# Value products placed between the matmuls of the Fourier transforms, two width groups in later rows, and value fetches on ScalarE in five rows of eight

## The chip, the cores and the metric

The kernel runs on one core of a Trainium2 chip. The metric is the device time of one execution in microseconds; the median of several runs is given. Before the change it is 3284.2 us (three runs, 3283.5 to 3284.87 us).

The core has five engines with queues of their own: TensorE (PE in the profile; PEld are its weight loads), VectorE (DVE), ScalarE (ACT), GpSimd (POOL) and SyncE (SP), which here only issues DMAs.[...]

## The reference, cut to what matters

The input x has the shape (32, 56, 56, 128): 32 images, 56 by 56 tokens, 128 channels, all in fp32. Two layers follow, each added to its input after a group norm:

```python
x = x + window_attention(group_norm(x))     # layer 0
x = x + fourier_ff(group_norm(x))           # layer 1

# window_attention: 7x7 windows, shifted by 3, 4 heads of 32 channels
qkv  = win @ w_qkv.T
attn = softmax(q @ k.T * scale + bias + mask)
out  = (attn @ v) @ w_proj.T + b_proj

# fourier_ff
out_y = einsum(dct(x along W)[:32 modes], w0)
out_x = einsum(dct(x along H)[:32 modes], w1)
h     = idct(out_x along H) + idct(out_y along W)
out   = relu(h @ W1 + b1) @ W2 + b2
```

The product attn @ v is what this document calls the values. dct(..) with 32 modes is the forward transform, idct the back transform; both are matmuls with constant matrices.

## The kernel before, in words

**Rows and cycles.** The kernel goes through the images in rows of windows: NWR = 8 rows an image, 256 rows in all. One turn of the outer loop (line 1219) is a cycle. In cycle r, attention's scores are made for row r, and values and projection for row r - 3; the softmax of the rows between runs on VectorE, GpSimd and ScalarE meanwhile. Eleven cycles after an image's first row (CONV_BEGIN = 11), its second layer begins. It is spread over 16 cycles, counted by c, which the text calls steps: in every cycle one image is at a step c from 0 to 7 and, where there is an earlier one, this is at step c + 8 (`fourier`, line 905). Cycles before 11 (`first_rows`) fill this pipeline.

**What each step of the second layer does.** Step 0: forward transform over the width, two halves h of the tokens (`transform`, lines 688 to 710). Steps 1 and 2: forward transform over the height, one half each, in two pieces. Steps 3 to 5: mixing of the modes by w1 and w0 (`mix`). Then the back transform in groups of 16 lines (`modes_back`, line 777), the last group with 8: `back_groups` (line 910) gives height groups 0 and 1 to step 5, 2 and 3 to step 6, width groups 0 and 1 to step 7, 2 and 3 to step 8. Each group is fetched from PSUM by `fetch_back`: height groups by ScalarE copies into xf, width groups by VectorE additions onto xf. Steps 8, 9, 10 and 12 to 15 are the feed-forward layer, in seven groups of up to 512 tokens (FF_AT, `ff_in`, `ff_out`).

**Order inside a cycle.** The order on PE, ScalarE, VectorE and GpSimd is written by hand (line 1201): the instructions stand on each engine as the Python code calls them. A steady cycle calls `halves_first` (qk products, first feed-forward matmuls), `half_columns` (mixing), `eighths` (values, then the forward transform), `quarters` (scores; the back transform after them where a feed-forward group runs in the same cycle, else before), `attn_max`, `last_fetch`, and `halves_last` (the v product of this row, rest of the mixing, exp, `ff_out`, projection). So on PE a steady cycle reads: qk, feed-forward in, values, forward transform, scores, back transform, v, mixing, feed-forward out, projection.

**How the matmuls sit in the array.** Tokens lie in two halves of the 128 partitions. A value product (line 546) has 49 rows, in the upper or lower row half u, and 32 columns for its head h: eight places. It is made for four pairs of windows pr, so a row has 32 value products. They run with pr outside, then h, then u, so that the halves alternate. A transform product (line 702) has 56 rows in row half r and 32 columns for its block g of channels, again eight places, r innermost. A product of the back transform (line 789) has 64 rows (li) and 64 columns (hs): four places; a group has four chunks c (the last group two), each with four products. Scores (line 477) have 64 by 64 too. All other matmuls use 128 rows and 64 columns. In the profile each fp32 product counts as two matmuls.

**Banks.** PSUM has four banks named pa for attention and four named pc for the second layer, each taken in turn. The values take two banks (po), one for each u; two banks later in turn v and the projection come to them again. ScalarE fetches u = 0 (one instruction), VectorE u = 1 (three, because of the shifted window), in lines 560 to 578. Each transform and each group of the back transform takes two pc banks.

**Loads.** `load_back` (line 915) issues on SP the loads of zT for the back groups of the next cycle; `load_columns` (line 732) those of the token columns for the height transform.

Of the kernel before, what the change touches and what calls it, by code (L numbers as in the profile page):

```python
# [1 line left out]

# [1 line left out]

# [11 lines left out]
S = 56  # L16
C = 128
WS = 7
SS = 3
NH = 4  # L20
HD = C // NH
WT = WS * WS
NWR = S // WS
# [10 lines left out]
JP = 64  # L34
# [13 lines left out]
def swin_fourier_kernel(  # L48
# [33 lines left out]
    def attn_bank():  # L82
        return bank("pa", 4)
# [447 lines left out]
        nc.vector.transpose(eT.rearrange("p t (k j) -> p k t j", k=2), blocks[r % 2])  # L531
        im.eT[i] = eT

    def attn_values(im, i, r):


        v = v_sb[r % 3]
        po = [attn_bank(), attn_bank()][::-1]
        HALF = RT // 2
        po4 = [p[:, :HALF].rearrange("p (r n s) -> p n r s", r=WS, s=WS) for p in po]  # L540
        eT = im.eT.pop(i)
        for pr in range(NP):
            for h in range(NH):
                for u in range(2):
                    ks = slice(u * JP, u * JP + WT)
                    nc.tensor.matmul(  # L546
                        po4[u][h * HD : (h + 1) * HD, pr],
                        lhsT=v[ks, pr, h * HD : (h + 1) * HD],
                        rhs=eT[ks, h * NP + pr, :WT],
                        start=True,  # L550
                        stop=True,
                    )

        if i % 2 == 0:
            im.oT = oT_sb[i // 2 % 2]
        oT = im.oT


        oTr = oT[:, i % 2 * RT : (i % 2 + 1) * RT].rearrange("p (r x) -> p r x", x=S)
        for u in range(2):  # L560
            src = po[u][:, :HALF].rearrange("p (r f x) -> p r f x", r=WS, f=NP)
            n = NP - u
            dst = bass.AP(
                oTr.tensor,
                oTr[:, :, SS + u * WS :].offset,
                [oTr.ap[0], [S, WS], [2 * WS, n], [1, WS]],
            )
            parts = [(dst, src[:, :, :n])]
            if u:
                parts += [  # L570
                    (oTr[:, :, S - WS + SS :], src[:, :, n, : WS - SS]),
                    (oTr[:, :, 0:SS], src[:, :, n, WS - SS :]),
                ]
            for d, f in parts:
                if u:
                    nc.vector.tensor_scalar(d, f, im.bias[:, 2:3], None, ALU.add)  # L576
                else:
                    nc.scalar.activation(d, f, AF.Identity, bias=im.bias[:, 2:3])  # L578
# [109 lines left out]
    def transform(im, width, h):  # L688

        if width:  # L690
            toks = [x1[:, 2 * CH * h : 2 * CH * (h + 1)]]
        else:
            toks = [im.cols.pop(2 * h + j) for j in range(2)]
        dct_sb = (dct_w if width else dct_h)[:, :, 0]
        py = [conv_bank(), conv_bank()]
        at = 0
        for tok in toks:
            n = tok.shape[1] * KB
            for g in range(C // KB):
                cs = slice(g * KB, (g + 1) * KB)  # L700
                for r, ps in enumerate(LINE):
                    nc.tensor.matmul(  # L702
                        py[r][cs, at : at + n],
                        lhsT=dct_sb[ps],
                        rhs=tok[ps, :, cs],
                        start=True,
                        stop=True,
                    )
            at += n
        im.py[width, h] = py  # L710

    def turn_modes(im, width, h):

# [63 lines left out]
    def modes_back(im, width, g):  # L777

        if not width and g == 0:
            im.xf = big.tile([P, S, S], F32, tag="xf", name="xf", bufs=2)  # L780
        zT = im.zT.pop((width, g))
        idct = idctw if width else idcth.rearrange("p h r -> p (h r)")
        l0, n = LINES[g]
        nch = n // 4
        px = [conv_bank(), conv_bank()]
        for c in range(nch):
            for li, ls in enumerate(HALVES):
                for hs in HALVES:
                    nc.tensor.matmul(  # L789
                        px[li][hs, c * 2 * S : (c + 1) * 2 * S],  # L790
                        lhsT=zT[ls, c, hs],
                        rhs=idct[ls, :],
                        start=True,
                        stop=True,
                    )
        im.px[width, g] = px

    def fetch_back(im, width, g):

# [109 lines left out]

    def back_groups(c):  # L910

        if c in (5, 6, 7, 8):
            return [(c >= 7, (c + 1) % 2 * 2 + j) for j in range(2)]
        return []

    def load_back(cycle):
        for im, c in fourier(cycle):
# [75 lines left out]
    def has_ff(cycle):  # L993
        return any(c in FF_AT for _, c in fourier(cycle))
# [9 lines left out]
                for g in (2 * c - 8, 2 * c - 7):  # L1004
                    mix(im, True, g)

    def quarters(cycle):
        def back():
            for im, c in fourier(cycle):
                for j, (width, g) in enumerate(back_groups(c)):  # L1010
                    modes_back(im, width, g)
                    if not (c == 8 and j):
                        fetch_back(im, width, g)

        if not has_ff(cycle):
            back()
        im, i = row(cycle)
        if im:
            attn_scores(im, i, cycle)
        if has_ff(cycle):  # L1020
            back()

    def eighths(cycle):
        im, i = row(cycle - 3)
        if im:
            attn_values(im, i, cycle - 3)
        for im, c in fourier(cycle):
            if c == 0:
                for h in range(2):
                    transform(im, True, h)  # L1030
                    turn_modes(im, True, h)
                next(im.stats)
            if c == 1:
                for r in range(2):
                    scale_modes(im, True, 1, r)
                shift_modes(im, True)
            if c in (1, 2):
                transform(im, False, c - 1)
                if c == 1:
                    for g in range(2):  # L1040
                        load_columns(im, g + 2)

    def last_fetch(cycle):
        for im, c in fourier(cycle):
            if c == 8:
                fetch_back(im, *back_groups(c)[1])

    def columns_turn(cycle):
        for im, c in fourier(cycle):
# [60 lines left out]
                ff_out(im, FF_AT.index(c))  # L1110

    EARLY = (0, 3, 4, 5, 7)

    def halves_last(cycle):
        im, i = row(cycle)
# [29 lines left out]
    def first_rows(cycle):  # L1145
        im, i = row(cycle)
        im3, i3 = row(cycle - 3)
        if im:
            attn_qk(im, i)
        if cycle == NWR:  # L1150
            norm_step(cycle)
        last, j = row(cycle - 4)
        if last:
            attn_sums(last, j)
        if cycle >= NWR:
            next_quarter(cycle)
        if cycle:
            attn_exp(cycle - 1)
        if im3:
            attn_values(im3, i3, cycle - 3)  # L1160
        tokens_bias(cycle)
        if im:
            attn_scores(im, i, cycle)
            attn_max(cycle)
        if last:
            attn_squares(last, j)
            add_sums(last, j)
        divide(cycle)
        turn(cycle)
        if im3:  # L1170
            attn_project(im3, i3)
        if cycle in (0, NWR - 1):
# [12 lines left out]
        next_groups(cycle)  # L1185
        if cycle == NWR - 2:
            for _ in range(2):
                norm_step(NWR - 1)
        if 1 < cycle < 10:
            mix_weights(cycle - 2)  # L1190
        if cycle in (6, 7):
            back_weights(cycle - 6)
        if cycle == 8:
            ff_weights()
        if cycle == CONV_BEGIN - 1:
            attn_sums(im3, i3)
            attn_squares(im3, i3)
            attn_exp(cycle)

    ET = mybir.EngineType  # L1200
    with tc.manual_schedule(engines={ET.PE, ET.Activation, ET.DVE, ET.Pool}):
# [17 lines left out]
        for cycle in range(NB * NWR + CONV_BEGIN + FF_AT[-1] - NWR + 1):  # L1219
# [4 lines left out]
            if not row(cycle - 3)[0]:  # L1224
                eighths(cycle)
                columns_turn(cycle)
                behind_max(cycle)
                half_columns(cycle)
                half_columns(cycle, True)
                scale_first(cycle, 0)  # L1230
                scale_first(cycle, 1)
                load_first(cycle)
                last_out(cycle)
                quarters(cycle)
# [6 lines left out]
            quarters(cycle)  # L1241
            if row(cycle)[0]:
                attn_max(cycle)
            last_fetch(cycle)
# [66 lines left out]
```

## Time and profile before

| what | value |
|---|---|
| median of three runs | 3284.2 us (3283.5 to 3284.87) |
| the profiled execution | 3282.72 us, its span 3280.9 us |
| mean granted TensorE clock | 0.991 |
| value products, L546 | 16384 matmuls, busy 209.3 us |
| forward transform, L702 | 3072 matmuls, busy 59.3 us (width) and 72.9 us (height) |
| back transform, L789 | 7168 matmuls, busy 107.1 us (width) and 99.6 us (height) |
| scores, L477 | 8192 matmuls, busy 234.5 us |
| VectorE fetch of values, L576 | 768 instructions, 171.5 us |
| ScalarE fetch of values, L578 | 256 instructions, 117.2 us |

The busy time of a group of matmuls is that of the union of its instructions, whose ends are modelled, so it is no measure of how well the array is filled. A row of a steady cycle takes about 3280.9 us over 256 rows, some 12.8 us, the fill and the end of the pipeline included. A line of the timeline gives the start, the time from the first start to the last end, engine, line, operation and tiles, and the number of instructions.

### The profile page before, as it was taken

What the parts mean: (1) busy time and instruction counts of PE and PEld (TensorE: products, weight loads), DVE (VectorE), ACT (ScalarE), POOL (GpSimd) and SP (SyncE); (2) the same over time, 40 slices, a digit from 0 to 9 for tenths busy, and PEclk for the clock granted to TensorE, in tenths of its full rate; (3) what the DMA queues carried; (4) which work ended last, traced back from release to release, by engine and by line L of the source; (5) the groups of instructions that cost most, each with busy time, mean ns of one, the idle gap of its engine ahead of it and who ended that gap; (6) DMA issues with size and microseconds to landing.
All of it is one profiled execution on the core that took longest, in us unless ns stands there. A gap on an engine that the chain in (4) does not pass through costs nothing.

```text
span 3280.9 us, 151050 instructions
## 1 busy us (share of the span) xinstructions
PE 3154.8 (96%) x65408; PEld 2394.1 (73%) x65408; DVE 2637.5 (80%) x5066; ACT 2100.4 (64%) x3680; POOL 2346.8 (72%) x2634
## 2 busy tenths in 40 slices
PE   4689999999999999999999999999999999999999
PEld 3467777777777777777777777777777777777776
DVE  8788888888888888888888888888888888888751
ACT  3456766666766666666666766666666666666663
POOL 7777777777777677777777777777777777777741
PEclk9799999999999999999999999999999999999999
DMA  6546556565556555656556656656565656565453
GB/s 115 106 119 147 137 138 144 136 143 146 137 134 142 137 142 143 142 135 146 137 144 145 141 134 143 137 141 144 136 140 136 146 131 146 140 143 136 121 140 96
DMA packets 1168157, 448.39 MB, mean 137 GB/s; under 512 B 520106, under 2 KB 1137628, under 8 KB 1167492
## 3 DMA queue, kind: packets, MB, share of 16 engines
q1 hardware_dynamic: 1158148, 433.18, 55.7%
q8 instruction: 514, 8.42, 1.1%
q10 hardware_dynamic: 8736, 5.38, 0.7%
q14 instruction: 151, 1.24, 0.1%
q0 software_dynamic: 608, 0.17, 0.0%
HBM read 276.97 MB, written 161.48 MB: 134 GB/s over the span
## 4 chain that ended last, share of the span: by engine, by line
PE 83%; ACT 7%; DVE 3%; DMA 2%; issue 2%; SPq 2%; POOL 0%; ACTq 0%; DVEq 0%; POOLq 0%
PE pc L113 38%; PE pa L113 10%; PE pa L455 7%; PE pc L789 5%; PE pa L591 5%; PE pc L750 5%; PE pa L477 5%; PE pa L546 4%; PE pc L702 3%; ACT hid L833 2%; ACT k L442 2%; SPq L760 1%; ACT xr L628 1%; ACT z L758 1%; DMA zscr<-z 1%
## 5 line engine op out<-in xcount | busy, mean ns | idle before, releaser
L521 POOL TENSOR_TENSOR blocks<-a,rs 128x512 f32<-128x512 f32 x1506 | 1280.5, 857 | 399.2 <-DVE rs L509 251.2
L113 PE MATMUL pc<-wff,hid 128*64 128x128 f32 x12544 | 742.0, 273 | 2.6 <-ACT hid L833 1.0
L113 PE MATMUL pc<-xf,wff 128*64 128x512 f32 (+2 forms) x3584 | 718.5, 539 | 1.0 <-DVE xf L807 0.9
L113 PEld LDWEIGHTS pc<-wff,hid 128*64 128x64 f32 x12544 | 706.5, 137 | 15.7 <-ACT hid L833 5.3
L496 POOL TENSOR_TENSOR a<-a,mx 128x784 f32<-128x784 f32 x251 | 377.7, 1505 | 358.6 <-DVE mx L495 341.6
L113 PEld LDWEIGHTS pc<-xf,wff 128*64 128x64 f32 x3584 | 278.6, 136 | 356.8 <-issue 249.6
L833 ACT ACTIVATE hid<-pc,b1sb 128x512 f32<-128x512 f32 (+2 forms) x896 | 500.5, 643 | 41.1 <-PE pc L113 41.1
L113 PE MATMUL pa<-xw,wn 128*64 128x392 f32 x2048 | 399.9, 501 | 29.6 <-ACT wn L411 29.6
L462 ACT COPY v<-pa 128x512 f32<-128x512 f32 x256 | 151.9, 593 | 414.7 <-PE pa L455 411.7
L485 DVE TENSOR_TENSOR a<-pa,bm 128x392 f32<-128x392 f32 x502 | 260.0, 559 | 90.2 <-PE pa L477 70.8
L442 ACT ACTIVATE k<-pa,bqkv,heads 128x392 f32<-128x392 f32 x512 | 319.0, 674 | 14.9 <-PE pa L113 1.1
L840 POOL TENSOR_TENSOR res<-res,b2sb 128x512 f32<-128x512 f32 (+2 forms) x256 | 265.7, 1044 | 85.0 <-DMA res<-scr 85.0
L725 ACT ACTIVATE y<-modes,rstd 128x448 f32<-128x448 f32 x256 | 276.3, 1137 | 71.5 <-DVE modes L718 64.0
L531 DVE STREAM_TRANSPOSE eT<-blocks 128x1024 f32<-128x1024 f32 x256 | 313.4, 1224 | 0.9 <-POOL blocks L521 0.9
L502 ACT ACTIVATE a<-a 128x784 f32<-128x784 f32 x251 | 214.9, 856 | 151.1 <-POOL a L496 150.9
L455 PE MATMUL pa<-wn,xw 128*64 128x128 f32 x4096 | 289.1, 283 | 22.0 <-ACT oT L578 16.4
L127 POOL TENSOR_TENSOR xr<-xr,bproj 128x384 f32<-128x384 f32 (+1 forms) x256 | 292.6, 1143 | 20.6 <-DMA xr<-in_x_dram 7.9
L546 PEld LDWEIGHTS pa<-eT,v 49*32 49x32 f32 x16384 | 173.6, 106 | 161.1 <-ACT hid L833 48.7
L432 ACT ACTIVATE q<-pa,bqkv 128x392 f32<-128x392 f32 x256 | 149.3, 583 | 220.7 <-PE pa L113 219.0
L576 DVE TENSOR_SCALAR oT<-pa,bqkv 128x147 f32<-128x147 f32 (+2 forms) x768 | 171.5, 279 | 140.5 <-PE pa L546 138.3
L507 DVE TENSOR_REDUCE sm<-a 128x16 f32<-128x784 f32 x251 | 240.9, 960 | 40.2 <-ACT a L502 40.1
L591 PE MATMUL pa<-wproj,oT 128*64 128x128 f32 x3584 | 249.9, 275 | 23.3 <-DVE oT L576 21.1
(108 smaller groups left out, 4975.3 us busy)
## 6 DMA issues: line engine op xcount, KB each, us to landing
zscr<-z SPq DMA_DIRECT2D x512, 112.0 KB
xin<-in_x_dram SPq DMA_DIRECT2D x496, 112.0 KB
htok<-scr SPq DMA_DIRECT2D x256, 196.0 KB
zT<-zscr SPq DMA_DIRECT2D x192, 256.0 KB
res<-scr SPq DMA_DIRECT2D x160, 256.0 KB
out_dram<-res SPq DMA_DIRECT2D x160, 256.0 KB
scr<-x SPq DMA_DIRECT2D x256, 112.0 KB
xr<-in_x_dram SPq DMA_DIRECT2D x256, 84.0 KB
```

Source lines behind the costliest of these rows:

```text
L113: nc.tensor.matmul(dst[ps], lhsT=lhsT[:, ps], rhs=rhs, start=start, stop=stop)
L127: nc.gpsimd.tensor_tensor(piece, piece, bproj.unsqueeze(1).to_broadcast([P, n, C]), ALU.add)
L442: nc.scalar.activation(k_sb[:, u], pk[:, :RT].rearrange("p (w j) -> p w j", j=WT), AF.Identity, bias=im.bias[:, 3 + u : 4 + u], scale=head ...
L455: nc.tensor.matmul(pv[HALVES[w % 2], w // 2 * C : (w // 2 + 1) * C], lhsT=im.half[i // NP][:, t0 : t0 + JP], rhs=im.w[:, 2 * C : 3 * C], s ...
L496: nc.gpsimd.tensor_tensor(a3, a3, mx.unsqueeze(2).to_broadcast([P, 2 * NWR, WT]), ALU.subtract)
L521: nc.gpsimd.tensor_tensor(dst[to, k, :, :n], a3[src, :, kb * KB : kb * KB + n], rs[src].unsqueeze(2).to_broadcast([src.stop - src.start, 2 ...
L531: nc.vector.transpose(eT.rearrange("p t (k j) -> p k t j", k=2), blocks[r % 2])
L546: nc.tensor.matmul(po4[u][h * HD : (h + 1) * HD, pr], lhsT=v[ks, pr, h * HD : (h + 1) * HD], rhs=eT[ks, h * NP + pr, :WT], start=True, sto ...
L591: nc.tensor.matmul(pp[hs, (n - n0) * C : (n - n0 + 1) * C], lhsT=oT[:, t0 : t0 + JP], rhs=wproj, start=True, stop=True,)
L725: nc.scalar.mul(y[:, r], t.rearrange("p (n k) -> p n k", k=NM), im.rstd)
L833: nc.scalar.activation(hf[:, :n], ph[:, :n], AF.Relu, bias=b1sb[:, f : f + 1])
L840: nc.gpsimd.tensor_tensor(im.res[:m, c0:c1], im.res[:m, c0:c1], b2sb[:m].unsqueeze(1).to_broadcast([m, c1 - c0, C]), ALU.add,)
```

## The change

Four things are changed.

1. Values, forward transforms and back transforms no longer run their own loops: each returns its products as two lists, one for each row half, of parts. A new function `beside` emits them: a part of the other work on row half 0, then value products on row half 1, then the other work on row half 1, then value products on row half 0, until the first piece of the other work is through. What remains follows in the old manner, one part at a time and both halves of it. Where there is no other work, all values are emitted with u = 1 ahead of u = 0. How many pairs of windows go into one place depends on the parts of the first piece: four (all) beside the width transform, two beside a half of the height transform and beside the short last back group, one beside a full back group.
2. The back transform is therefore called ahead of the scores in all rows. Width groups 2 and 3 leave step 8 and go one each to steps 11 and 12, where they are fetched in `last_fetch`; the second group of step 7 is fetched there too.
3. The value fetches are emitted after all of these products. In rows with cycle % 8 of 2, 3, 5, 6 or 7, which are steps 7, 0, 2, 3 and 4, ScalarE fetches both halves (four instructions), in the order 0, 1; in the others VectorE's three for u = 1 come first. The half u = 0 now has the first of the two banks.
4. Turning and scaling of modes, and the loads of the columns of step 1, follow both pieces instead of standing between them.

```diff
-    def attn_values(im, i, r):
+    def values(im, i, r):
         v = v_sb[r % 3]
-        po = [attn_bank(), attn_bank()][::-1]
+        po = [attn_bank(), attn_bank()]
...
-        for pr in range(NP):
-            for h in range(NH):
-                for u in range(2):
-                    ks = slice(u * JP, u * JP + WT)
-                    nc.tensor.matmul(
...
+        def product(u, pr, h):
+            ks = slice(u * JP, u * JP + WT)
+            nc.tensor.matmul(
...
+        return [
+            [[partial(product, u, pr, h) for h in range(NH)] for pr in range(NP)]
+            for u in range(2)
+        ]
+
+    def fetch_values(im, i, both=False):
...
-        for u in range(2):
+        for u in (0, 1) if both else (1, 0):
...
-                if u:
+                if u and not both:
                     nc.vector.tensor_scalar(d, f, im.bias[:, 2:3], None, ALU.add)
                 else:
                     nc.scalar.activation(d, f, AF.Identity, bias=im.bias[:, 2:3])
...
+        return [
+            [[partial(product, j, r, g) for g in range(C // KB)] for j in range(len(toks))]
+            for r in range(2)
+        ]
...
+        return [
+            [[partial(product, c, li, hs) for hs in HALVES] for c in range(nch)]
+            for li in range(2)
+        ]
...
     def back_groups(c):
 
-        if c in (5, 6, 7, 8):
-            return [(c >= 7, (c + 1) % 2 * 2 + j) for j in range(2)]
-        return []
+        if c in (5, 6, 7):
+            return [(c == 7, (c + 1) % 2 * 2 + j) for j in range(2)]
+        return [(True, c - 9)] if c in (11, 12) else []
...
+    def beside(mine, others):
+
+        def emit(parts):
+            for part in parts:
+                for product in part:
+                    product()
+
+        n = max(len(other[0]) for other in others) if others else 0
+        steps = [(other, k) for other in others for k in range(len(other[0]))]
+        if not mine:
+            for other, k in steps:
+                for r in range(2):
+                    emit(other[r][k : k + 1])
+            return
+        first = len(others[0][0]) if others else 0
+        if n == 1:
+            steps, first = steps, 1
+        share = NP // first if first else NP
+        for k in range(first):
+            other, at = steps[k]
+            emit(other[0][at : at + 1])
+            emit(mine[1][k * share : (k + 1) * share])
+            emit(other[1][at : at + 1])
+            emit(mine[0][k * share : (k + 1) * share])
+        if not first:
+            for pr in range(NP):
+                for u in (1, 0):
+                    emit(mine[u][pr : pr + 1])
+        for other, k in steps[first:]:
+            for r in range(2):
+                emit(other[r][k : k + 1])
 
     def eighths(cycle):
-        im, i = row(cycle - 3)
-        if im:
-            attn_values(im, i, cycle - 3)
+        last, i = row(cycle - 3)
+        mine = values(last, i, cycle - 3) if last else []
+        others = []
+        for im, c in fourier(cycle):
+            if c == 0:
+                others += [transform(im, True, h) for h in range(2)]
+            if c in (1, 2):
+                others.append(transform(im, False, c - 1))
+            for width, g in back_groups(c):
+                others.append(modes_back(im, width, g))
+        beside(mine, others)
+        if last:
+            fetch_values(last, i, cycle % NWR in VALUES_BY_ACT)
...
+            if c in (5, 6, 7):
+                for width, g in back_groups(c)[: 1 if c == 7 else 2]:
+                    fetch_back(im, width, g)
 
     def last_fetch(cycle):
         for im, c in fourier(cycle):
-            if c == 8:
-                fetch_back(im, *back_groups(c)[1])
+            if c in (7, 11, 12):
+                fetch_back(im, *back_groups(c)[-1])
...
+    VALUES_BY_ACT = (2, 3, 5, 6, 7)
```

More of the change, by code (lines that the diff above doesn't have):

```diff
@@ L1 @@
 from contextlib import ExitStack
+from functools import partial
 import numpy as np
@@ L541, in attn_values @@
         eT = im.eT.pop(i)
-        for pr in range(NP):
-            for h in range(NH):
-                for u in range(2):
-                    ks = slice(u * JP, u * JP + WT)
[L546 to L552, printed above, removed]
+        im.po = po
+        def product(u, pr, h):
+            ks = slice(u * JP, u * JP + WT)
+            nc.tensor.matmul(
+                po4[u][h * HD : (h + 1) * HD, pr],
+                lhsT=v[ks, pr, h * HD : (h + 1) * HD],
+                rhs=eT[ks, h * NP + pr, :WT],
+                start=True,
+                stop=True,
+            )
+        return [
[3 more added lines that the diff above has]
+    def fetch_values(im, i, both=False):
+        po = im.po
+        HALF = RT // 2
         if i % 2 == 0:
@@ L695, in transform, with product @@
         py = [conv_bank(), conv_bank()]
-        at = 0
-        for tok in toks:
+        im.py[width, h] = py
+        def product(j, r, g):
+            tok, ps, cs = toks[j], LINE[r], slice(g * KB, (g + 1) * KB)
             n = tok.shape[1] * KB
[L699 to L710, printed above, removed]
+            nc.tensor.matmul(
+                py[r][cs, j * n : (j + 1) * n],
+                lhsT=dct_sb[ps],
+                rhs=tok[ps, :, cs],
+                start=True,
+                stop=True,
+            )
+        return [
+            [[partial(product, j, r, g) for g in range(C // KB)] for j in range(len(toks))]
+            for r in range(2)
+        ]
     def turn_modes(im, width, h):
@@ L785, in modes_back, with product @@
         px = [conv_bank(), conv_bank()]
[L786 to L795, printed above, removed]
-        im.px[width, g] = px
+        im.px[width, g] = px
+        def product(c, li, hs):
+            nc.tensor.matmul(
+                px[li][hs, c * 2 * S : (c + 1) * 2 * S],
+                lhsT=zT[HALVES[li], c, hs],
+                rhs=idct[HALVES[li], :],
+                start=True,
+                stop=True,
+            )
+        return [
+            [[partial(product, c, li, hs) for hs in HALVES] for c in range(nch)]
+            for li in range(2)
+        ]
     def fetch_back(im, width, g):
@@ L1005, in half_columns, with scores @@
                     mix(im, True, g)
[L1007 to L1016, printed above, removed]
+    def scores(cycle):
         im, i = row(cycle)
@@ L1019, in quarters @@
             attn_scores(im, i, cycle)
-        if has_ff(cycle):
-            back()
-    def eighths(cycle):
-        im, i = row(cycle - 3)
-        if im:
-            attn_values(im, i, cycle - 3)
+    def beside(mine, others):
[27 more added lines that the diff above has]
+                emit(other[r][k : k + 1])
+    def eighths(cycle):
+        last, i = row(cycle - 3)
[11 more added lines that the diff above has]
+            fetch_values(last, i, cycle % NWR in VALUES_BY_ACT)
         for im, c in fourier(cycle):
@@ L1029, in eighths @@
                 for h in range(2):
-                    transform(im, True, h)
                     turn_modes(im, True, h)
@@ L1036, in eighths @@
                 shift_modes(im, True)
[L1037 to L1041, printed above, removed]
+                for g in range(2):
+                    load_columns(im, g + 2)
+            if c in (5, 6, 7):
+                for width, g in back_groups(c)[: 1 if c == 7 else 2]:
+                    fetch_back(im, width, g)
     def last_fetch(cycle):
         for im, c in fourier(cycle):
-            if c == 8:
-                fetch_back(im, *back_groups(c)[1])
+            if c in (7, 11, 12):
+                fetch_back(im, *back_groups(c)[-1])
     def columns_turn(cycle):
@@ L1159, in first_rows @@
         if im3:
-            attn_values(im3, i3, cycle - 3)
+            beside(values(im3, i3, cycle - 3), [])
+            fetch_values(im3, i3)
         tokens_bias(cycle)
@@ L1233, in swin_fourier_kernel @@
                 last_out(cycle)
-                quarters(cycle)
                 last_fetch(cycle)
@@ L1240, in swin_fourier_kernel @@
             eighths(cycle)
-            quarters(cycle)
+            scores(cycle)
             if row(cycle)[0]:
```

## The prediction, made before the changed kernel was run

> **What bounds the kernel now.** I read the page first, then the list of waits on PE, then the timeline of PE inside single rows, because the page says that PE decides and only the timeline shows how its stages follow each other. From the page:
>
> ```profile
> PE 3154.8 (96%) x65408; PEld 2394.1 (73%) x65408; DVE 2637.5 (80%) x5066; ACT 2100.4 (64%) x3680; POOL 2346.8 (72%) x2634
> PE   4689999999999999999999999999999999999999
> ...
> PEclk9799999999999999999999999999999999999999
> ...
> PE 83%; ACT 7%; DVE 3%; DMA 2%; issue 2%; SPq 2%; POOL 0%; ACTq 0%; DVEq 0%; POOLq 0%
> ```
>
> PE is busy in nine tenths or more of every slice after the third, at full granted clock, and carries 83% of the chain of waits. PE is idle 126 us in all (3280.9 - 3154.8), most of it in the first three slices. What is left in the steady part is small; the list of waits names it:
>
> ```profile
> PE pa L113 <- ACT wn L411: 29.6, 2, 24.4
> ...
> PE pa L455 <- ACT oT L578: 16.4, 30, 1.0
> ```
>
> The first line is the start. The second comes once an image (30 times, 0.55 us each), in the row of Fourier step 4, where the v product waits until ScalarE has fetched the values out of its bank. So a microsecond more or less of PE work in a row is nearly a microsecond of the span, and the question is what the new order of matmuls costs on PE. The timeline of PE in one row of step 7 (values L546, scores L477, back transform L789, v L455):
>
> ```profile
> 1591.82 0.81 PE L546 MATMUL pa<-eT,v 49*32 49x49 f32 x64
> 1592.56 0.91 PE L477 MATMUL pa<-k,q 64*64 64x98 f32 x32
> 1593.28 1.71 PE L789 MATMUL pc<-idctw,zT 64*64 64x112 f32 x64
> 1594.92 1.09 PE L455 MATMUL pa<-wn,xw 128*64 128x128 f32 x16
> ```
>
> "49*32" is rows times columns of the array that a matmul holds. Compare each start with the modelled end (start plus length) of the line above. Scores and back transform are both 64*64: the second starts 0.19 us before the first ends. Values to scores is 64x32 to 64x64 (49 rows lie in a half of 64), back to v is 64x64 to 128x64: there the next starts only 0.07 us before the end. The values and the forward transform (L702) have one size, and run into each other; the transform and the scores do not:
>
> ```profile
> 1603.55 0.76 PE L546 MATMUL pa<-eT,v 49*32 49x49 f32 x61
> 1604.11 0.56 PE L702 MATMUL pc<-x,dct_w 56*32 56x448 f32 x1
> 1604.12 0.20 PE L546 MATMUL pa<-eT,v 49*32 49x49 f32 x1
> 1604.12 0.56 PE L702 MATMUL pc<-x,dct_w 56*32 56x448 f32 x1
> 1604.14 0.22 PE L546 MATMUL pa<-eT,v 49*32 49x49 f32 x2
> 1604.16 1.77 PE L702 MATMUL pc<-x,dct_w 56*32 56x448 f32 x30
> 1605.86 0.91 PE L477 MATMUL pa<-k,q 64*64 64x98 f32 x32
> ```
>
> Transform matmuls start in rounds of eight, 376 ns apart, for 448 columns: 0.84 ns a column. With that rate I took, over the whole trace, the time from the end of the last matmul's streaming to the start of the next stage. Where the size stays it is zero or below (-36 ns from values to transform). Where it changes it is 92 to 96 ns at the median, every time: 157 changes from values to scores 92 ns, 93 from transform to scores 92 ns, 192 from 128x64 to values 96 ns. And it is the whole array that waits: the first scores matmul sits on the upper left quarter, the last transform matmul on the last columns of the lower half, and the scores still wait for that one.
>
> [...]the first scores matmul after a change is 295 ns long and later ones 243 (52 ns exposed for 64 columns), the first value matmul 228 against 203 (25 ns for 32). [...]above, transform matmuls start before the last value matmuls, so something here passes others on other tiles.[...]
>
> **The change, part by part.**
>
> *Back transform and values, interleaved.* In rows of step 5, 6, 7, 3 and 4 the new order is: two back products on row half 0 (64x64), values on row half 1 (64x32), two back products on half 1, values on half 0, and again. Every hand-over changes the size, so nothing lies beside anything. The length of such a piece:
> - Two back products are four matmuls (each fp32 product is two[...]). Exposed load 53 ns, two rounds of 94 ns (112 columns at 0.84), 7 ns for the second product's later start (starts in a round are 6.7 ns apart), 92 ns change: 340 ns with rounding.
> - Four value products: 25 ns load, two rounds of 41 ns, 20 ns for four starts, 92 ns: 220 ns (222 taken).
> - One step is two of each: 1.124 us; four steps are 4.50 us.
>
> Before, the same work took 0.735 us (values with the change after it, 1591.82 to 1592.56) and eight rounds of 95 ns, 0.76 us (one group of the back transform). So such a row grows by 4.50 - 0.735 - 0.76 = 3.00 us. The second group of steps 5 to 7 follows in one piece, as before. Step 4 has the short group (two chunks): two steps, with eight value products a piece (some 313 ns: four value rounds), 2 x 2 x (0.340 + 0.313) = 2.61 us, before 0.735 + 0.38; it grows by 1.50 us. Values of another image run beside steps 5 to 7 of 31 images and beside steps 3 and 4 (reached a whole image later) of 30: 31 x 3 x 3.00 + 30 x (3.00 + 1.50) = 279 + 135 = +414 us.
>
> *Transform and values, interleaved.* One size, so the two halves can work at once. Step 0: before, 2.22 us (1603.55 to 1605.86 less the change). After, each half has two transforms of 2 x 0.376 and its values, 4 x 0.082, in a row, some 1.9 to 2.0 us with the starts: -0.25 us. Steps 1 and 2: before, 1.65 us (1618.20 to 1619.94 less 0.09); after, 4 x 0.188 + 0.33 = 1.08 a half, 1.35 with starts and instruction supply: -0.3 us each. 31 x 0.85 = -26 us. From both sides: nothing excludes that the values wait behind the transform's second pass; then the pieces lie one after another (rival 3).
>
> *Two width groups moved from step 8 to steps 11 and 12.* The same matmuls, and two fetches by VectorE (612 ns each, 375 for the short one), in rows where PE decides as well: nothing by itself. Their users come later: tokens 1536 to 2047 are used in step 12, and tokens from 2560 in step 14. The loads of zT, two a group on SP, go one group a row; in steps 5 to 7 the first group is wanted some 1.5 us sooner after its issue (5.3 us instead of 6.8 in the row above). The back transform waited for such a load 0.5 us in the whole run; I take nothing, up to 20 us. The loads of htok for step 1 are issued behind both pieces of values; SP has no wait before PE's list.
>
> *Values fetched by ScalarE in five rows of eight.* VectorE loses three instructions, 371 + 237 + 230 = 0.84 us; ScalarE gains three, at 458 ns for 196 elements and 342 ns for 56 (L578, L730) some 1.1 us, about 170 us in all. What stands behind them on ScalarE is v's copy (L462), which waited 414.7 us for PE: they are covered. The v product now waits for the first fetch alone (0.46 us), under the scores' 0.73 us. Cost nothing; without the cover up to 0.6 us in 160 rows.
>
> *A wait that goes.* In step 4's row ScalarE gets 1.5 us more before v is due: the 16.4 us go, and nothing is late next, PE being the later one.
>
> Sum: 414 - 26 - 16 = +372 us on 3282.7 us (the profiled execution; its span is 3280.9), 3654; the median of the runs is 1.5 us above, so **3655 us**.
>
> **The rivals.**
> 1. *Clock falls.* An interleaved stretch is 4.5 us long and PE streams in half of it, on half the array. The clock record moves in steps of 3.41 us; reckoned as streaming time, steps with 0.39 or less were followed by half clock, steps with 0.42 or more were not. Half of the time is above; counted by array area it would be a quarter, below. Then some 0.72 of 123 rows would lose 1.7 to 3.4 us: 3805 to 3955, middle 3880 us.
> 2. *The other side: no drain between different halves.* If the change of size costs only where tiles overlap, values and back run beside each other: 1.09 + 0.09 us a row instead of 1.495, -0.31 us. 31 x 3 x 0.31 + 30 x 0.62 = 47, with 26 of the transforms: 3284 - 73 = 3211 us. It decides where a step of two back and two value pieces takes under 0.374 us (1.495 over 4), against 1.124. For it: no hand-over of before is between disjoint tiles alone. Against: the scores' start above waits for a disjoint tile.
> 3. *Transform and values don't overlap.* Step 0 gains 0.7 us instead of losing, steps 1 and 2 0.77 each: 31 x (2.24 + 0.85) = +96 us, 3750 us.
>
> **How the numbers follow.** Chances: the forecast 0.68, clock 0.16, no overlap 0.08, no drain 0.07, no measurable change 0.01. The forecast's own range is 3600 to 3710 (10 ns on each of 123 x 16 changes are 20 us; the transforms' gain may be 0 to 1.5 us an image; ScalarE's waits may stay). The range to 3840 takes in rival 3 and the low end of rival 1. A difference of 0.2%, 6.6 us, is what can be told from none: faster 0.07, within 0.01, slower 0.92.
>
> **What would show it.** Right: in the timeline of a step 5 row, sixteen alternating groups of L789's and L546's successors of about 0.34 and 0.22 us, 4.5 us together, rows of steps 0 to 2 slightly shorter, granted clock still 0.99, and more VectorE and ScalarE idle time in rows of steps 3 to 7 that ends with PE. Wrong: back and value matmuls that start within each other's groups (rival 2); PEclk under 9 in all slices (rival 1); transform groups that start only after the value group ended (rival 3).

## The result, and the profile after

The changed kernel takes 3924.5 us (median of four runs, 3921.5 to 3929.4); the kernel before, run beside it, 3284.5 us. The ratio is 1.195, with a 95% interval of 1.193 to 1.196. The direction was forecast and the size was not: 3655 us, with a range up to 3840, were predicted. The profiled execution has a span of 3922.8 us against 3280.9, and a mean granted clock of 0.925 against 0.991.

The page of the kernel after, the lines that answer to those shown of before (line numbers have moved: values L545, back transform L799, scores L478, v L456, forward transform L709):

```profile
PE 3805.6 (97%) x65408; PEld 2767.9 (71%) x65408; DVE 2503.6 (64%) x4601; ACT 2217.7 (57%) x4145; POOL 2341.7 (60%) x2634
...
PE   4699999999999999999999999999999999999999
...
PEclk9899999999899989899999999998998998989989
```

PE has as many instructions as before and is as full, over a span that is 642 us longer. VectorE lost 134 us of work and ScalarE gained 117; with PE as the bound neither shows in the time. What is new is the third line: the granted clock dips again and again, where before it stood at 9 from the third slice on. The trace's clock record, which lists the stretches at full and at half clock, has 592 us at half clock, before 64 us.

The timeline of PE in a row of step 5 that fell wholly into full clock:

```profile
1494.67 0.41 PE L799 MATMUL pc<-idcth,zT 64*64 64x112 f32 x4
1495.01 0.29 PE L545 MATMUL pa<-eT,v 49*32 49x49 f32 x8
1495.23 0.41 PE L799 MATMUL pc<-idcth,zT 64*64 64x112 f32 x4
1495.57 0.29 PE L545 MATMUL pa<-eT,v 49*32 49x49 f32 x8
1495.79 0.41 PE L799 MATMUL pc<-idcth,zT 64*64 64x112 f32 x4
...
1499.15 1.00 PE L799 MATMUL pc<-idcth,zT 64*64 64x112 f32 x32
1499.97 0.85 PE L478 MATMUL pa<-k,q 64*64 64x98 f32 x32
```

These are single instructions merged into groups: first the back transform's piece on one row half, then the values on the other, and so on. Read the starts: 0.34 us from a back piece to a value piece, 0.22 us to the next back piece, 1.12 us for a step of two and two (1494.67 to 1495.79). No interleaved group starts inside another by more than the 0.07 us that stands for a full stop. Over the whole trace the median pause, from the end of the last matmul's streaming to the next start, reckoned as in the prediction, is 93 ns from back transform to values (1104 times) and 92 ns from values to back transform (1044 times). That these lie on different row halves helps nothing.

The granted clock, in stretches that are steps of the clock record, around the next row of step 5, whose interleaved stretch begins at 1608.14 (columns: stretch, its length, PE busy and instructions, granted clock, DMA share, GB/s):

```profile
1605.71:1609.12 3.41, 3.41 (x35) 1.00 0.51 133
1609.12:1612.53 3.41, 3.41 (x80) 1.00 1.21 172
1612.53:1615.94 3.41, 3.41 (x76) 0.50 0.06 12
1615.95:1619.36 3.41, 3.41 (x66) 1.00 0.05 14
```

The second stretch holds short pieces only, and the third runs at half clock, though PE's modelled busy time is full in all four. And the list of waits has a new line:

```profile
PE pc L799 <- ACT hid L847: 25.2, 59, 0.8
```

The back transform now comes straight behind the feed-forward products and needs the banks which ScalarE still reads there; before, the values stood between. The line of step 4, v behind ScalarE's oT, is down from 16.4 us to 0.3.

### The profile page after: what moved, and what is told of

Its sections match the earlier page's. It is cut to its first block, busy times and chain, and to the rows that moved or that the text cites. A ratio compares the mean times of both kernels' runs of the same rounds, so it can differ in the third digit from the quotient of the medians.

```text
span 3922.8 us, 150807 instructions
## 1 busy us (share of the span) xinstructions
PE 3805.6 (97%) x65408; PEld 2767.9 (71%) x65408; DVE 2503.6 (64%) x4601; ACT 2217.7 (57%) x4145; POOL 2341.7 (60%) x2634
## 5 line engine op out<-in xcount | busy, mean ns | idle before, releaser
L114 PE MATMUL pc<-wff,hid 128*64 128x128 f32 x12544 | 752.2, 276 | 1.9 <-issue 0.8
L114 PEld LDWEIGHTS pc<-wff,hid 128*64 128x64 f32 x12544 | 722.7, 139 | 9.4 <-ACT hid L847 3.8
L586 ACT ACTIVATE oT<-pa,bqkv 128x196 f32<-128x196 f32 (+3 forms) x721 | 205.7, 361 | 642.9 <-PE pa L545 642.9
L545 PE MATMUL pa<-eT,v 49*32 49x49 f32 x16384 | 520.1, 218 | 11.6 <-DVE eT L532 6.3
L114 PEld LDWEIGHTS pc<-xf,wff 128*64 128x64 f32 x3584 | 268.7, 136 | 366.8 <-issue 298.6
L545 PEld LDWEIGHTS pa<-eT,v 49*32 49x32 f32 x16384 | 315.1, 108 | 240.1 <-issue 76.1
L456 PE MATMUL pa<-wn,xw 128*64 128x128 f32 x4096 | 351.1, 326 | 0.7 <-issue 0.3
L799 PE MATMUL pc<-idctw,zT 64*64 64x112 f32 x3584 | 319.9, 315 | 17.0 <-ACT hid L847 17.0
L456 PEld LDWEIGHTS pa<-wn,xw 128*64 128x64 f32 x4096 | 279.7, 165 | 40.8 <-issue 11.2
L799 PE MATMUL pc<-idcth,zT 64*64 64x112 f32 x3584 | 296.2, 321 | 10.1 <-ACT hid L847 8.2
```

The lines of the kernel that those rows point to most:

```text
L114: nc.tensor.matmul(dst[ps], lhsT=lhsT[:, ps], rhs=rhs, start=start, stop=stop)
L456: nc.tensor.matmul(pv[HALVES[w % 2], w // 2 * C : (w // 2 + 1) * C], lhsT=im.half[i // NP][:, t0 : t0 + JP], rhs=im.w[:, 2 * C : 3 * C], s ...
L545: nc.tensor.matmul(po4[u][h * HD : (h + 1) * HD, pr], lhsT=v[ks, pr, h * HD : (h + 1) * HD], rhs=eT[ks, h * NP + pr, :WT], start=True, sto ...
L799: nc.tensor.matmul(px[li][hs, c * 2 * S : (c + 1) * 2 * S], lhsT=zT[HALVES[li], c, hs], rhs=idct[HALVES[li], :], start=True, stop=True,)
```

## The experiments

Ten kernels were run, each beside the kernel before. The edits are against the kernel after, if nothing else is said, and are cut to the lines that matter; where `backs` stands, it is a second list that takes the back transform's pieces.

**Which interleaving costs: the back transform apart.**

```diff
-                others.append(modes_back(im, width, g))
+                backs.append(modes_back(im, width, g))
         beside(mine, others)
+        beside([], backs)
```

> The back transform's products are emitted in one piece after the values; the forward transforms stay interleaved, everything else as after the change. Theory A (each hand-over between 64x64 and 64x32 drains the whole array, and the short half-array pieces then bring the granted clock to half for part of the time): the drains and the half clock go, what is left is the interleaving of the forward transforms (step 0 about 0.77 us longer an image, 24 us) less the wait of 16 us that goes: 3285 to 3315 us, clock 0.99. Rival B (the cost comes from the back transform standing ahead of the scores, with its banks and fetches, not from the alternation): it stands there still, so well above 3500 us. Rival C (the forward transforms' interleaving is a large part of the loss): above 3400 us.

Measured: 3275.9 us, ratio 0.997 (0.996 to 0.998), clock 0.989, a little below what theory A gave (later runs put that down to the moved width groups). Nearly all of the loss lies in the alternation of back transform and values. Rivals B and C are out.

**The reverse: only the back transform interleaved.**

```diff
-        beside(mine, others)
+        beside(mine, backs)
+        beside([], others)
```

> The reverse: the back transform stays interleaved with the values, the forward transforms follow the values in one piece. Theory A: only the 24 us of the forward transforms go, and perhaps some half clock in the row of step 0: 3870 to 3905 us, half clock still over 500 us of the span. Rival C: under 3750 us.

Measured: 3871.6 us, ratio 1.179 (1.177 to 1.180), 527 us at half clock. 53 us below the kernel after, inside the range but twice the 24 of the forward transforms. The rest goes with 65 us less at half clock, net in rows of steps 3 and 6 (3.3 us against 4.2, and 3.9 against 5.1, an image, counted from a row's first qk matmul), whose order is the same in both kernels; why they differ is open.

**Nothing interleaved.**

```diff
-        beside(mine, others)
+        beside(mine, [])
+        beside([], others)
+        beside([], backs)
```

> Nothing is interleaved: values, then the forward transform or the back transform in one piece, then scores. What remains of the change is the place of the width groups 2 and 3 (steps 11 and 12), the back transform ahead of the scores in all rows, and the fetches on ScalarE in five rows. Theory A: these cost nothing and remove up to 16 us of PE waits: 3265 to 3290 us. Rival B: well above 3400 us.

Measured: 3250.5 us, ratio 0.990 (0.988 to 0.991): better than both kernels, and below the expected range: the gain is more than the waits that were counted. Against it the interleaving of the forward transforms alone (3275.9) costs 25 us. The timeline of PE in its rows of steps 3 and 4:

```profile
1625.75 0.81 PE L545 MATMUL pa<-eT,v 49*32 49x49 f32 x64
1626.49 1.00 PE L799 MATMUL pc<-idctw,zT 64*64 64x112 f32 x32
1627.31 0.85 PE L478 MATMUL pa<-k,q 64*64 64x98 f32 x32
1628.09 1.09 PE L456 MATMUL pa<-wn,xw 128*64 128x128 f32 x16
...
1636.51 0.81 PE L545 MATMUL pa<-eT,v 49*32 49x49 f32 x64
1637.24 0.61 PE L799 MATMUL pc<-idctw,zT 64*64 64x112 f32 x16
1637.68 0.85 PE L478 MATMUL pa<-k,q 64*64 64x98 f32 x32
1638.46 1.09 PE L456 MATMUL pa<-wn,xw 128*64 128x128 f32 x16
```

In step 3, values and back transform together take 1.56 us (1625.75 to 1627.31); interleaved at full clock they took 4.48.

**Is it the size, or the alternation? The back transform in 32 columns.** Each of its products is made as two of 32 columns, so that both have one size in the array.

```diff
-            [[partial(product, c, li, hs) for hs in HALVES] for c in range(nch)]
+            [[partial(product, c, li, slice(k, k + KB)) for k in range(0, C, KB)] for c in range(nch)]
```

> All interleaving as after the change, but each 64x64 product of the back transform is made as two products of 32 columns, so that back transform and values have one size in the array; twice the matmuls in the back transform, the same result. Theory A: no change of size between them, so pieces on different row halves run beside each other: the stretch of step 5 falls from 5.3 us to 2 to 2.7 us, the clock stays at 0.99, total 3250 to 3350 us. Rival B, and any reading in which alternating between the halves is what costs: above 3700 us.

Measured: 3496.3 us, ratio 1.065 (1.063 to 1.066), clock 0.987: above what theory A gave, far below rival B. The start of an interleaved row:

```profile
1665.22 0.30 PE L799 MATMUL pc<-idcth,zT 64*32 64x112 f32 x4
1665.25 0.29 PE L545 MATMUL pa<-eT,v 49*32 49x49 f32 x8
1665.35 0.29 PE L799 MATMUL pc<-idcth,zT 64*32 64x112 f32 x8
1665.44 0.23 PE L545 MATMUL pa<-eT,v 49*32 49x49 f32 x4
```

With one size the pieces do start inside each other: values 0.03 us after the first back matmul, the next back piece 0.10 us later. The pauses of 93 and 92 ns are gone, and the half clock is down to 95 us, from 592. But the gain that was to follow is absent: in rows that nothing disturbs, step 3 takes 1.69 us against 1.56 apart, step 5 2.58 against 2.32. And most rows of steps 5 to 7 have a stop of 0.8 to 2.6 us (59 stops in 93 rows), at changing places:

```profile
PE pa L478 <- issue: 49.3, 33, 2.6
PE pc L799 <- issue: 46.9, 32, 2.3
```

"issue" is a wait for nothing that the profile shows; in the kernel before, all such waits before the back transform were 7.7 us. This kernel has 14 thousand instructions more (165113 in all against 150807). The part on DMA queues of the page has a queue q8 with packets of 16 KB, called instructions there, and its count rises with them (packets, MB, share; first the kernel before, then this one):

```profile
q8 instruction: 514, 8.42, 1.1%
q8 instruction: 569, 9.32, 1.2%
```

The trace ties the stops to these packets. Of the 89 stops of over 0.4 us after the first 300 us, 86 end 1.2 to 1.75 us after one of them has landed, where a moment taken at random has a chance of 9% to lie so; in the kernel before it is 15 of 15. I read these stops as PE standing until its next instructions have come; that is a reading of these times and was not tried apart, nor what the rows would take without the stops. About 30 of the 246 us over the version apart I could not place.

**What brings the clock down: whole-array pieces.** With the forward transforms apart:

```diff
             emit(other[0][at : at + 1])
-            emit(mine[1][k * share : (k + 1) * share])
             emit(other[1][at : at + 1])
+            emit(mine[1][k * share : (k + 1) * share])
             emit(mine[0][k * share : (k + 1) * share])
```

> As the run with only the back transform interleaved (3872 us), but a piece takes both row halves: four back products, then eight value products, so that a row has 8 changes of size where it had 16, and each piece streams through the whole array. At full clock a step is 0.354 + 0.247 = 0.60 us, four of them 2.40 us against 1.56 us apart: 3250 + 123 x 0.85 + 30 x 0.2 = 3361 us. Theory A' (the clock falls when the share of array area that streams in one 3.41 us step of the clock record is under about 0.36; here it is 0.45): 3340 to 3380 us and under 110 us at half clock. Rival D (the half clock comes with the changes of size themselves, half as many here): about 300 us at half clock and 3450 us or more.

Measured: 3415.4 us, ratio 1.040 (1.038 to 1.041), 83 us at half clock, as much as in kernels without this interleaving (64 to 79). The steps come out as worked out, 0.60 us, four in 2.40 us. Half of the changes of size, and the surplus of half clock is gone whole: rival D is out for this kernel. The stretch is also shorter here (2.40 us against 4.48); the next run shortens it and keeps the half-array pieces. The time is above theory A's; 24.5 us are the wait for hid, left out of the expectation, and the rest lies in rows of steps 6 and 7, where the first piece also waits within itself for its second bank (it lasts 0.76 and 0.70 us there, 0.35 in step 5).

**The same halves and sizes, a shorter stretch.** With the forward transforms apart:

```diff
         share = NP // first if first else NP
+        first //= 2
...
-        if not first:
-            for pr in range(NP):
-                for u in (1, 0):
-                    emit(mine[u][pr : pr + 1])
+        for pr in range(first * share, NP):
+            for u in (1, 0):
+                emit(mine[u][pr : pr + 1])
```

> As the run with only the back transform interleaved, halves and sizes as there, but only the first half of the steps of a row are interleaved (two instead of four, one instead of two in step 4), the rest of the values and of the back transform follows in one piece each. The stretch of short pieces is 2.2 us instead of 4.5 us, less than one 3.41 us step of the clock record, so the share of streaming array area in such a step stays near (2.25 x 0.24 + 1.16 x 0.95) / 3.41 = 0.48. Full clock: each row 1.53 us over the version apart (step 4: 0.68), 3250 + 123 x 1.53 + 30 x 0.68 = 3459 us. Theory A': 3430 to 3480 us, under 110 us at half clock. Rival D (half clock in proportion to the changes of size): some 300 us at half clock, 3550 us.

Measured: 3496.9 us, ratio 1.065 (1.063 to 1.066), 153 us at half clock. In rows of steps 3, 4 and 5 there is none behind the fill of the pipeline. What is left over the usual 64 to 79 us lies in the row of step 7, 2.5 us an image, mostly a single step of the clock record; there PE waits half a microsecond for hid just before the stretch. Both theories miss: A' gave under 110 us, D 300.

**The same, each step beginning with the values.**

```diff
-            emit(other[0][at : at + 1])
             emit(mine[1][k * share : (k + 1) * share])
-            emit(other[1][at : at + 1])
+            emit(other[0][at : at + 1])
             emit(mine[0][k * share : (k + 1) * share])
+            emit(other[1][at : at + 1])
```

> As the half-interleaved run (3497 us, 153 us at half clock, nearly all of it in the row of step 7, one clock step an image), but each step begins with the values, so that the back transform does not wait for ScalarE's hid at the row's start. Theory A' (the PE wait of half a microsecond just before the stretch is what brought the share under the limit): the half clock of step 7 goes, half clock under 110 us, and with it the 24.5 us of waits: 3415 to 3455 us. Rival D (the half clock belongs to the changes of size): half clock stays near 150 us, 3465 to 3490 us.

Measured: 3467.8 us, ratio 1.055 (1.053 to 1.057), 119 us at half clock, waits for hid 10.1 us instead of 24.5. Between the two: the half clock in step 7 falls from 2.5 to 1.5 us an image and is not gone. So that wait probably has a part in it, though the order of the pieces changed with it; what the rest depends on is open.

**Where the version apart gains.** First, the version with nothing interleaved, without ScalarE's extra fetches:

```diff
-    VALUES_BY_ACT = (2, 3, 5, 6, 7)
+    VALUES_BY_ACT = ()
```

> As the version with nothing interleaved (3250.5 us), but VectorE fetches the half u = 1 of the values in all rows, as before the change. If the moved width groups are what makes that version faster than the kernel before: 3244 to 3257 us. If the fetches on ScalarE are: 3275 to 3290 us.

Measured: 3251.7 us, ratio 0.990 (0.988 to 0.991): the fetches are worth nothing either way. Then the kernel before with the width groups alone moved:

```diff
-        if c in (5, 6, 7, 8):
-            return [(c >= 7, (c + 1) % 2 * 2 + j) for j in range(2)]
-        return []
+        if c in (5, 6, 7):
+            return [(c == 7, (c + 1) % 2 * 2 + j) for j in range(2)]
+        return [(True, c - 9)] if c in (11, 12) else []
```

> The kernel before with one edit: width groups 2 and 3 of the back transform in steps 11 and 12 instead of 8, with their fetches. If that move is the gain of 35 us: 3244 to 3262 us. If the gain is in the fetches on ScalarE or in the order of back transform and scores: 3275 us or more.

Measured: 3254.6 us, ratio 0.990 (0.989 to 0.992). The gain is the move. At the median, from one row's first value product to the next row's, the row of step 0 gets 1.57 us shorter, that of step 3 only 0.62 us longer, and that of step 4 even 0.24 us shorter; over the whole run it is 0.98 us an image (30.4 us).

**Why the forward transforms gained nothing.** With the back transform apart, in step 0 the values in pieces of eight products beside both transforms:

```diff
-            steps, first = steps, 1
+            steps, first = steps, 2
```

> As the run with the back transform apart and the forward transforms interleaved (3276 us), but in step 0 the values go in pieces of eight products beside both transforms instead of pieces of sixteen beside the first. Theory E ([...]a piece of sixteen value products[...] blocks, in the trace after 24 of its 32 matmuls, a piece of eight does not): step 0 falls from 3.08 us to 1.9 to 2.3 us, total 3240 to 3258 us. Rival F (transform and values on different halves hardly run beside each other at all): step 0 stays at 3 us, 3270 to 3282 us.

Measured: 3256.2 us, ratio 0.991 (0.989 to 0.992), 20 us less than with pieces of sixteen. Step 0 takes 2.43 us instead of 3.08. Rival F is out; theory E's range for the step (1.9 to 2.3) is missed a little, and apart it takes 2.31. What happens with sixteen is seen in the kernel after, timeline of PE in step 0:

```profile
1904.73 0.58 PE L709 MATMUL pc<-x,dct_w 56*32 56x448 f32 x4
1904.76 0.46 PE L545 MATMUL pa<-eT,v 49*32 49x49 f32 x24
1905.13 0.56 PE L709 MATMUL pc<-x,dct_w 56*32 56x448 f32 x4
1905.32 0.65 PE L545 MATMUL pa<-eT,v 49*32 49x49 f32 x6
1905.78 0.56 PE L709 MATMUL pc<-x,dct_w 56*32 56x448 f32 x1
```

Of the 32 value matmuls of the first piece 24 start at once beside the transform. The transform on the other row half, next in the program, starts only at 1905.78, with the last of the piece, 1.05 us after the first transform. In that time its row half has nothing but those values to do, 0.33 us of streaming.

## Why the prediction was off

**Changes of size: right, and sized right.** A step of 1.124 us was predicted, 1.120 was measured; a stretch of four 4.50, measured 4.48; the short piece of step 4 2.61, measured 2.59. Lowest stage times at full clock, taken against the version with nothing interleaved: 31 x (2.98 + 2.98 + 2.90) for steps 5 to 7 and 30 x (2.93 + 1.41) for steps 3 and 4, together 405 us where the working had 414. The pause at a change of size, 92 to 96 ns in the trace before, stands between tiles on different row halves as well (93 and 92 ns), which the run with 32 columns shows from the other side: with one size the values start 0.03 us after the first back matmul. Rival 2 is out. (The sum itself, 3282.7 + 372 + 1.5, makes 3656; the 1 us changes nothing.)

**The clock: the step that failed.** The forecast's sum has no term for the clock. Rival 1 had the falls of the clock, their place and a range of 150 to 300 us, and a chance of 0.16. The parts are: 405 us for the changes of size, 24 for step 0, 25 for the waits on hid, less 35 for the version apart, 419; 642 were lost. The 223 left stand beside 528 us more at half clock (592 less 64), which would cost 264 if all of it were streaming. What it does cost can be read from rows of the same step in the trace after: in steps 3, 5, 6 and 7 a row is 0.44 us longer for each us that it spends at half clock (a fitted line within each step). 528 x 0.44 is 232, and with the 419 that makes 651 where 642 were lost.

The failed step is the reckoning that set the clock's term at nothing. It counted streaming as time, half of the stretch, and found the limit between 0.39 and 0.42, so that the stretch stood above it. I had named the other way, by area, and not worked it out. Done for each 3.41 us step of the trace before (each matmul's columns at 0.84 ns, times its share of the array), it separates better there already: the clock fell after steps of at most 0.29, and held after all of at least 0.40. The interleaved stretch has 0.24. In the kernel after the clock fell 102 times (without the first fall, ahead of the matmuls, and the one at the span's end), after steps of at most 0.38, and held after none under 0.35; counted as time, it fell after steps of up to 0.64 and held after one of 0.47. In the four other kernels with alternating or whole-array pieces the shares with and without a fall meet between 0.35 and 0.39; in the run with 32 columns it held after steps down to 0.31. So a limit, if there is one, is only roughly known. The runs on whole-array pieces and on half the steps say that it is not the number of changes. That the half clock follows the area exactly is a reading of the traces and not shown: two expectations built on it were missed by some 10 and 40 us of half clock. Nor did every fall come after an idle PE: its modelled busy time was 3.41 of 3.41 us in the step before the fall shown above; and of the twelve falls in the trace before only five came after a step with next to no streaming (0.03 of the time or less), the others after up to 0.39.

**Forward transforms: -26 us predicted, +25 measured.** In size rival 3 came true in step 0 (+0.77 us), though not by its reason, since 24 of 32 value matmuls do start beside the transform; steps 1 and 2 are even (1.69 us before, 1.67 after). The term assumed that each row half works off its own list. The traces show neither that nor a strict order of the program: in step 0 before, a transform matmul started at 1604.11 and value matmuls that stand ahead of it in the program at 1604.12 and 1604.14; but in the kernel after a piece of sixteen products held back what stood behind it (the next transform started 1.05 us after the first), and with pieces of eight the step was shorter (2.43 us against 3.08). That run also spreads the values over both transforms, so the length of the piece is the likely cause and not shown alone. Even then the interleaving gains nothing.

**Width groups: 0 predicted, -31 measured.** "By itself nothing" overlooked that the rows were not alike. In step 0 the two groups took 1.44 us (1606.59 to 1608.03 in the trace before), more than their twelve rounds of 95 ns (1.14). Of the two, the short one went into step 4, a row where v already waited on ScalarE; why that row even got shorter is open.

**ScalarE's fetches** cost nothing, as predicted, at 0.95 us a row (estimate 1.1). **The wait of step 4** went, as predicted; that a new one would come, 25 us for hid, at the start of rows which now begin with the back transform, was missed. For the start of these rows the prediction had weighed the loads of zT, and not the banks.

## What to carry to other kernels

Before matmuls are put beside each other on different parts of the array, look whether they have one size of tile: where they had not, each hand-over was a full stop here (92 to 93 ns, on different row halves too), and sixteen pieces in turn took 4.48 us where the same work apart took 1.56. With such short pieces on half the array the granted clock was at half for 592 us here, against 64 before, so work out the share of array area that streams in a step of the clock record, beside the share of time; here area told the falls better (at most 0.38 before a fall, at least 0.35 where the clock held, where time gave 0.64 and 0.47). And look in which row the bound engine waits before placing work that must be done anyway: moving two groups to other rows was worth 1% here with a few lines.

## What was not expected of the hardware

- Pieces of one size on two row halves did start inside each other (values 0.03 us after the first back matmul), and still interleaving gained nothing: 1.69 us against 1.56 in step 3, 2.43 against 2.31 in step 0.
- Half clock came in single and double steps of 3.41 us, 36 and 64 of 104 in the kernel after, with PE's modelled busy time at 100% in 95 of the 104; the busy row of the profile does not show these falls.
- Stops of PE with no releaser, up to 2.6 us each and 123 us in all, in the kernel with the most matmuls; 86 of the 89 over 0.4 us end 1.2 to 1.75 us after a packet of queue q8 has landed.
